# Power of the last group of roots ahead of a rounding, row of the scale from PSUM, late copies of b2 after the early products

## The chip, the cores and the metric

The kernel runs on one core of one Trainium2 chip. The metric is the device time of one execution in microseconds (us). A core has five engines with a queue each: TensorE (PE in the profile, with its weight loads as PEld), VectorE (DVE), ScalarE (ACT), GpSimd (POOL) and SyncE (SP), which here issues DMAs. An engine takes its instructions in order; an instruction that needs the result of another engine waits for a semaphore, and holds up what is queued behind it.

## The reference

```python
xn = _layernorm(x, axis=-1)                                  # x: 8 x 512 x 1024, float32
x = x + attn(xn, w1, w2, b2, sparse_mask) + ffn(xn, weight, bias)

def attn(x, w1, w2, b2, sparse_mask):
    a = jnp.einsum('ds,td->st', w1, w2) * sparse_mask
    y = jnp.einsum('bds,st->bdt', x, a) + b2
    return jax.nn.gelu(y, approximate=False)

def ffn(x, weight, bias):
    w_scale = 448.0 / max(amax(abs(weight)), 1e-12)
    w_q = clip(weight * w_scale, -448, 448).astype(float8_e4m3fn)
    x_scale = 57344.0 / max(amax(abs(x)), 1e-12)
    x_q = clip(x * x_scale, -57344, 57344).astype(float8_e5m2)
    acc = jnp.einsum('bsk,nk->bsn', x_q.astype(float32), w_q.astype(float32))
    return acc * (1.0 / x_scale) * (1.0 / w_scale) + bias
```

The mask is nonzero only near the diagonal (within 70 columns of a block). Both amax values are taken over whole tensors: no row of x can be quantized before the largest normalized value of all 4096 rows is known.

## The kernel before

The 4096 rows are 32 tiles of 128 rows by 1024 columns. Tiles 0 to 15 are "early": they are loaded, normalized in place, transposed (L489), multiplied with the banded, masked attention matrix (L514) and put through gelu (L524) while the statistics and the largest value of all tiles are still being gathered. The last eight early tiles have their transposed copies in one large buffer (`xnt_big`). Tiles 16 to 31 are "late": in the first half they pass only for statistics (L310, or by ScalarE for tiles 16 to 23) and row maxima (L396, `row_max`), and are loaded again after it, normalized into a new tile (L382), transposed, multiplied and put through gelu (L536).

Two scales separate the halves. For each, named "w" and "x", `global_amax` (L706) runs five steps: `amax_rows` on VectorE (L407, one maximum per partition, `x_mine`), a transpose on TensorE into one PSUM row (L412, `pt_x`), `amax_row` on VectorE (L416 finds the largest value, `x_top`; L421 spreads it over a row of 128, `x_row`), a transpose back to 128 partitions on TensorE (L424), and `scale_and_inverse` on VectorE (L428 to L431). x's chain starts once the reciprocal roots of the variances of all groups of tiles are there. The last group, tiles 28 to 31, takes three steps: `variance` on VectorE (L333, `var`), `power` on GpSimd (L337, `r`), and `inverse_root` on VectorE (L343 to L345: `t`, `t`, `rstd`), with `shifts` (L348) behind it; then `late_amax` (L436) scales the row maxima.

The weight is eight chunks of 128 by 1024. Once w's scale is known, ScalarE scales a chunk (L450), VectorE makes a "magic" number for each element (L456, L459), whose addition and subtraction round to three bits, and GpSimd adds and subtracts it, half a chunk at a time (`weight_rounded`: L468 and L469). Chunks 6 and 7 are rounded by VectorE instead (L463, L464).

After both scales are known, VectorE quantizes a transposed tile (L547), TensorE multiplies it with the rounded weight (L554), and VectorE applies scale and bias and adds the rest (L566, L569, L578). 

PSUM holds four tiles of 512 columns for the masked products (`py`), two for the linear part and attention matrix, two for transposes. b2 comes into a `py` tile before the products: by a copy on ScalarE (`preload`, L505) or, for early tiles 11 to 15, by a bias matmul on TensorE (`b2_matmul`, L509). A `py` tile comes free with its gelu. All other tiles of 128 by 1024 come from a pool of 34 slots; an instruction that writes into a slot waits for the last reader of what was there.

The order of the instructions is made by a planner (`Plan`, L116): each step is given an engine, a cost, a rank, the steps that it comes after, and slots that it takes and frees; the planner plays this through in time and emits the steps in the order in which they start. The costs are numbers written by hand, so the plan is not the execution; but each engine's queue has the plan's order.

The lines that the change touches are these, and what they name: `root[TILES - 1]` is the `inverse_root` step of the last group, `products[i]` the last product matmul of early tile i, `rows_op` the step that splits b2 for the bias matmul.

Of the kernel before, what the change touches and what calls it, by code (L numbers as in the profile page):

```python
# [14 lines left out]
ALU = mybir.AluOpType  # L15
AX = mybir.AxisListType

P = 128
# [3 lines left out]
TILES = NT // P  # L22
GROUP = 8
EARLY = 16
# [20 lines left out]
AMAX_EPS = 1e-12  # L45
# [70 lines left out]
class Plan:  # L116
# [8 lines left out]
    def do(self, engine, cost, rank, emit, *args, lag=0.2, after=(), take=(), free=()):  # L125
        after = [op for op in after if op is not None]
        op = Op(engine, cost, rank, lag, after, take, free, emit, args)
        self.ops.append(op)
        return op
# [47 lines left out]
def banded_path(  # L177
# [12 lines left out]
    nc = tc.nc  # L190
# [54 lines left out]
    v = {}  # L245
# [168 lines left out]
    def amax_top(name):  # L414
        v[name, "top"] = top = const.tile([1, 1], F32, name=f"{name}_top")
        nc.vector.tensor_reduce(top, v[name][:1, 0, :], AX.X, ALU.max)  # L416

    def amax_row(name):
        amax_top(name)
        v[name, "row"] = row = const.tile([1, P], F32, tag="amax_row", name=f"{name}_row")  # L420
        nc.vector.tensor_scalar_max(row, v[name, "top"].to_broadcast([1, P]), AMAX_EPS)  # L421

    def amax_back(name):
        nc.tensor.transpose(v[name][:, 1, 0:1], v[name, "row"], ident[:1, :1])  # L424
# [189 lines left out]
    for k in range(4):  # L614
        y = ps_y.tile([P, HALF], F32, tag="y", name=f"py_first_{k}")
# [3 lines left out]
    do = plan.do  # L619
    LOAD, T, V, A, G = "load", "tensor", "vector", "scalar", "gpsimd"  # L620
# [26 lines left out]
    b2_op = do(G, 0.6, 1, load_b2, lag=12.0, after=(attn_ops[0],))  # L647

    attn_mm, attn_ready = [], []
    for sc in range(NC):  # L650
        mm = do(
            T, 3.5, sc * 0.1, attn_matmuls, sc, after=[attn_ops[c] for c in range(sc + 1)],
            take=("f",), free=("slot",),
# [7 lines left out]
    root, shifted = {}, {}  # L661
# [7 lines left out]
    for lo, hi in GROUPS:  # L669
        group = [stat[i] for i in range(lo, hi)]  # L670
        if 0 < lo and hi < TILES:
            op = do(G, 1.7 + 0.16 * (hi - lo), 0, inverse_root_gpsimd, lo, hi, after=group)
        else:
            op = do(V, 0.2, 0, variance, lo, hi, after=group)
            op = do(G, 0.4 + 0.16 * (hi - lo), 0, power, lo, hi, after=(op,))
            op = do(V, 0.6, 0, inverse_root, lo, hi, after=(op,))
        for i in range(lo, hi):
            root[i] = shifted[i] = op
        if lo == 0 or hi == TILES:
            op = do(V, 0.2, 0 if lo == 0 else 99, shifts, lo, hi, after=(op,))  # L680
# [11 lines left out]
    for i in range(EARLY, TILES):  # L692
# [6 lines left out]
        after=[maxima[i] for i in SQUARED] + [root[i] for i in SQUARED],  # L699
# [3 lines left out]
        after=[squared] + [maxima[i] for i in range(TILES)] + [root[i] for i in range(TILES)],  # L703
    )

    def global_amax(name, fp8_max, rank, cols, after, lag=0.1):  # L706
        op = do(V, 0.2, rank, amax_rows, cols, name, after=after, lag=lag)
        op = do(T, 0.4, rank, amax_transpose, name, after=(op,), take=("t",))
        op = do(V, 0.5, rank, amax_row, name, after=(op,))
        op = do(T, 0.3, rank, amax_back, name, after=(op,))  # L710
        return do(V, 0.5, rank, scale_and_inverse, name, fp8_max, after=(op,), free=("t",))
# [6 lines left out]
    rows_op = do(G, 8.6, 2, b2_parts, after=(b2_op, normal[11]))  # L718
    w_known = global_amax("w", E4M3_MAX, 0, w_cols, sums)
    rounded, for_vector = [], []  # L720
    for c in range(NC):
        op = do(A, 1.1, 1, weight_scaled, c, after=(w_known, w_twice[c]))
        op = do(V, 1.4, 1, weight_magic, c, after=(op,), take=("magic",))
        if c in ROUNDED_BY_VECTOR:
            for_vector.append((c, op))
            continue
        op = do(G, 2.55, 1, weight_rounded, c, 0, after=(op, rows_op))
        rounded.append(
            do(G, 2.55, 1, weight_rounded, c, 1, after=(op,), free=("slot", "magic", "twice"), lag=4.0)
        )  # L730
# [7 lines left out]
    products, added = {}, {}  # L738
    evicted = {}
    for i in range(EARLY):  # L740
        in_big = i >= EARLY - NC
        for q in range(2):
            op = do(
                T, 0.52, 10 * i - 11 + q, transposes, i, q,
                after=(settled[i], attn_mm[NC - 1] if in_big else None, evicted.get((i, 0))),
                take=("t",) if in_big or q else ("t", "slot"),
            )
# [10 lines left out]
        op = evicted[i, 1]  # L758
        ends = []
        for piece in band_pieces():  # L760
            op = do(
                T, 0.4, 10 * i, product_matmul, i, *piece, lag=0.1 if not piece[-1] else 0.2,
                after=(op, evicted[i, 0], attn_ready[piece[0]], pre[piece[1]]),
            )
# [4 lines left out]
        op = do(LOAD, 2.5, 200 + 10 * i, lambda: None, lag=0.0, after=(*ends, late))  # L769
# [11 lines left out]
    normal_late, evicted_late, pre_late, added_late = {}, {}, {}, {}  # L781
    last_piece = {}
    for n, j in enumerate(range(EARLY, TILES)):
        s = step[n]
        fetched[j] = do(
            LOAD, 1.4, 195 + 10 * n, load_x, j, lag=2.0, take=("slot", "late"), after=(maxima[j],)
        )
        xn = do(A, 1.2, 100 + s, normalize_late, j, after=(fetched[j], shifted[j], known if n > 1 else root[TILES - 1]), take=("slot",))
        if n == 0:
            for q in range(2):  # L790
                op = do(
                    T, 0.52, 900 + q, transposes, j, q, after=(xn, evicted_late.get((j, 0))),
                    take=("t",) if q else ("t", "slot"), free=("slot",) if q else (),
                )
                evicted_late[j, q] = do(A, 0.55, 50, evict_transposed, j, q, after=(op,), free=("t",))
        normal_late[j] = xn
        for h in range(2):
            pre_late[j, h] = do(A, 0.55, 60 + s, preload, j, h, after=(b2_op,), take=("y",))
    linear = None
    for s, k in enumerate(steps):  # L800
        rank = 1000 + 10 * s
        j = EARLY + k if k < EARLY else None
        if j is not None:
            quantized[k] = do(
                V, 1.3, 100 + s, quantize, k, after=(x_known, products[k], evicted[k, 1]),
                take=("quant",), free=("slot",) if k < EARLY - NC else (),
# [4 lines left out]
        op = linear  # L811
        sums_k = []
        for kind, args in interleaved(j is not None, nxt is not None):
            if kind == "product":
                h = args[1]
                op = do(
                    T, 0.33, rank, product_matmul, j, *args, lag=0.0,
                    after=(op, evicted_late[j, 0], evicted_late[j, 1], pre_late[j, h]),
                )
                if args[-1]:  # L820
                    last_piece[j, h] = op
            elif kind == "transpose":
                c, = args
                q, first, last = c // (NC // 2), c % (NC // 2) == 0, c % (NC // 2) == NC // 2 - 1
                op = do(
                    T, 0.13, rank, transpose_one, nxt, c, lag=0.0, after=(op, normal_late[nxt]),
                    take=(("t", "slot") if c == 0 else ("t",)) if first else (),
                    free=("slot",) if c == NC - 1 else (),
                )
# [4 lines left out]
            else:  # L834
                h, c = args
                op = do(
                    T, 0.215, rank, linear_matmul, k, h, c, lag=0.0,
                    after=(op, quantized[k], *(rounded if s == 0 else ())),
                    take=("f",) if c == 0 else (), free=("quant",) if (h, c) == (1, NC - 1) else (),
                )  # L840
# [3 lines left out]
        if j is not None:  # L844
            for h in range(2):
                g = do(
                    A, 0.55, 20 + s, gelu_late, j, h, after=(last_piece[j, h],),
                    take=() if h else ("slot",), free=("y",),
# [6 lines left out]
                take=("quant",), free=("slot",),  # L855
            )
        totals = []
        for h in range(2):
            ready = added_late[k, h] if k >= EARLY else added[k]
            if s == TILES - 1:  # L860
                op = do(G, 1.27, 20 + s, add_bias, k, h, after=(ready, bias_op))
                op = do(V, 0.8, 10 + s, total_at_once, k, h, after=(op, sums_k[h], known), free=("f",))
# [11 lines left out]
    for sc in range(NC):  # L874
        m = do(
            LOAD, 1.4, 300 + sc, load_mask, sc, lag=2.0, take=("slot", "stream"),
            after=(known, stored[2 * sc + 3]),
# [4 lines left out]
    op = do(V, 0.2, 300, amax_rows, out_cols, "o", after=checks)  # L882
    op = do(T, 0.3, 5000, amax_transpose, "o", after=(op,), take=("t",))
# [248 lines left out]
def layernorm_masked_product_fp8_linear(tc, x, w1, w2t, b2, mask, wt, bias, out):  # L1132
    nc = tc.nc
    with tc.tile_pool(name="flag", bufs=1) as pool:
        flag = pool.tile([1, 1], I32, name="flag")
        banded_path(tc, x, w1, w2t, b2, mask, wt, bias, out, flag)
        general = nc.values_load(
            flag,
            min_val=0,
            max_val=1,  # L1140
            skip_runtime_bounds_check_because="a comparison gives 0 or 1",
        )
    with tc.If(general != 0):
        general_path(tc, x, w1, w2t, b2, mask, wt, bias, out)
# [35 lines left out]
```

## Time and profile before

| | us |
|---|---|
| median of 3 runs | 320.34 |
| the runs | 320.34, 320.46, 318.3 |
| the profiled execution | 318.67 |
| its span in the profile | 316.9 |
| TensorE busy | 291.6 |
| VectorE busy | 231.7 |
| ScalarE busy | 158.2 |
| GpSimd busy | 134.4 |

The profile is of one execution. A busy share is an average over stages: about 50 us of loading with the attention matrix and the first tiles, then until about 122 us the rest of the early tiles beside statistics, maxima and the weight's rounding, then the linear part of all tiles and the products of the late ones. In lines of the timelines the columns are start and length in us, engine, line of the kernel, operation, what is written and read with its shape, and the count; brackets give the engine's idle time just before, and what is taken to have ended it. In lines of waits: who waited for whom, the total, the number of times, and the longest. Matmuls are pipelined, so a matmul's own length overlaps the next one's; in the chain of waits each has only the time until the next one starts.

How the 40 slices of the span look (busy tenths of each engine):

```profile
PE   2779889998999979999999999999999999999992
DVE  3489698999999969646577677767767755766581
```

### The profile page before, as it was taken

Reading aid. Unit: us, or ns where it says so; the run is one execution under the profiler, and the core shown is the slowest. Engines: PE = TensorE matmul, PEld = TensorE weight load, DVE = VectorE, ACT = ScalarE, POOL = GpSimd, SP = SyncE. Lnnn points to the kernel's source line nnn. Section 1 sums busy time; section 2 is a strip of 40 time slices with the busy share of each in tenths; the row PEclk is TensorE's granted clock in tenths of the full one; section 3 lists DMA queues with packets and bytes.
Section 4 is the critical chain, followed back from the end, with each engine's and each line's share of the span. In section 5 each row is a group of like instructions: output and inputs, shape, how many; then the busy total and the mean of one; then the engine's idle time right before and its main releaser. Section 6 shows DMA issues by size and latency. Waiting matters only on the chain.

```text
span 316.9 us, 4342 instructions
## 1 busy us (share of the span) xinstructions
PE 291.6 (92%) x1555; PEld 217.9 (69%) x1555; DVE 231.7 (73%) x342; ACT 158.2 (50%) x255; POOL 134.4 (42%) x165
## 2 busy tenths in 40 slices
PE   2779889998999979999999999999999999999992
PEld 0757668896998867876676676676667667667650
DVE  3489698999999969646577677767767755766581
ACT  1368369584999973744344334523524443452110
POOL 3151708988488789666202311311330231131160
PEclk9999999999999998999999999999999999999999
DMA  7999999999535746999999986653153322221313
GB/s 248 407 383 378 391 392 390 395 420 418 222 110 221 238 161 112 208 209 271 296 283 299 379 334 223 243 186 147 66 199 133 115 109 114 103 96 66 134 67 141
DMA packets 28365, 73.74 MB, mean 233 GB/s; under 512 B 3376, under 2 KB 11568, under 8 KB 28336
## 3 DMA queue, kind: packets, MB, share of 16 engines
q1 hardware_dynamic: 20992, 47.17, 40.2%
q0 software_dynamic: 2592, 9.44, 14.7%
q10 hardware_dynamic: 4752, 16.78, 13.1%
q8 instruction: 14, 0.23, 0.3%
q14 instruction: 15, 0.12, 0.1%
HBM read 56.60 MB, written 16.78 MB: 232 GB/s over the span
## 4 chain that ended last, share of the span: by engine, by line
PE 61%; DVE 19%; DMA 10%; SPq 5%; POOL 1%; issue 1%; ACT 0%; DVEq 0%
PE pf L554 35%; PE py L514 21%; DMA w<-in_w_dram 8%; DVE row_amax L396 6%; PE pt L489 5%; SPq L259 4%; DVE st L310 4%; DVE magic L456 2%; DVE w_cols L444 2%; DMA x<-in_x_dram 2%; DVE magic L459 2%; SPq L250 1%; PE pa L293 1%; DVE mean_var L311 1%; DVE xnt_big L501 1%
## 5 line engine op out<-in xcount | busy, mean ns | idle before, releaser
L554 PE MATMUL pf<-wq,xqts 128*128 128x512 bf16 x512 | 149.5, 379 | 0.0
L514 PE MATMUL py<-attn,xnt 128*128 128x268 f32 (+2 forms) x480 | 117.3, 340 | 1.6 <-ACT py L505 0.9
L514 PEld LDWEIGHTS py<-attn,xnt 128*128 128x128 f32 x480 | 86.7, 190 | 24.1 <-ACT py L505 1.1
L539 POOL TENSOR_TENSOR x<-x,gelu 128x512 f32<-128x512 f32 x32 | 40.6, 1270 | 126.2 <-ACT gelu L536 124.7
L566 DVE SCALAR_TENSOR_TENSOR pf<-pf,descale,bias_bc 128x512 f32<-128x512 f32 x62 | 46.9, 756 | 54.2 <-PE pf L554 54.2
L554 PEld LDWEIGHTS <-xqts 128*128 128x128 fp8e5 x512 | 50.6, 101 | 23.6 <-issue 0.2
L536 ACT ACTIVATE gelu<-py 128x512 f32<-128x512 f32 x32 | 19.1, 597 | 76.5 <-PE py L514 73.1
L569 DVE TENSOR_TENSOR x<-pf,x 128x512 f32<-128x512 f32 x62 | 42.9, 692 | 4.4 <-DVE pf L566 0.5
L396 DVE TENSOR_REDUCE row_amax<-x 128x1 f32<-128x1024 f32 x32 | 37.6, 1201 | 4.5 <-POOL x L391 4.1
L293 PE MATMUL pa<-w_sb,w 128*128 128x268 f32 (+1 forms) x128 | 31.3, 402 | 9.5 <-DMA w_sb<-in_w2t_dram 9.5
L310 DVE BATCH_NORM_STATS2 st<-x 128x6 f32<-128x512 f32 x48 | 30.3, 673 | 8.2 <-DMA x<-in_x_dram 8.2
L293 PEld LDWEIGHTS pa<-w_sb,w 128*128 128x128 f32 x128 | 25.5, 207 | 14.8 <-issue 11.3
L498 ACT COPY xnt<-pt 128x512 f32<-128x512 f32 x48 | 27.2, 581 | 16.1 <-PE pt L489 16.1
L514 PE MATMUL py<-attn,xnt_big 128*128 128x198 f32 (+2 forms) x160 | 34.7, 353 | 0.0
L489 PE MATMUL pt<-ident,xn 128*128 128x128 f32 x128 | 33.9, 273 | 0.0
L505 ACT COPY py<-b_bc 128x512 f32<-128x512 f32 x54 | 31.9, 600 | 1.0
L514 PEld LDWEIGHTS py<-attn,xnt_big 128*128 128x128 f32 x160 | 27.5, 196 | 3.4 <-issue 0.8
L489 PEld LDWEIGHTS pt<-ident,xn 128*128 128x128 f32 x128 | 18.0, 141 | 13.9
L382 ACT ACTIVATE xn<-x,shift,rstd 128x1024 f32<-128x1024 f32 x16 | 19.9, 1241 | 11.1 <-DVE x L569 9.1
L524 ACT ACTIVATE x<-py 128x512 f32<-128x512 f32 x32 | 18.5, 600 | 11.2 <-PE py L514 11.1
L547 DVE TENSOR_SCALAR xqts<-xnt,x_scale 128x1024 fp8e5<-128x1024 f32 x24 | 21.2, 888 | 0.0
L489 PE MATMUL pt<-ident,x 128*128 128x128 f32 x128 | 18.8, 274 | 1.9 <-ACT xnt L498 0.9
(100 smaller groups left out, 236.2 us busy)
## 6 DMA issues: line engine op xcount, KB each, us to landing
x<-in_x_dram SPq DMA_DIRECT2D x48, 512.0 KB, 7.6
out_dram<-x ACTq DMA_DIRECT2D x31, 512.0 KB, 2.8
w<-in_wt_dram SPq DMA_DIRECT2D x16, 512.0 KB, 8.5
x<-in_x_dram POOLq DMA_DIRECT2D x16, 512.0 KB, 18.5
w<-in_w_dram SPq DMA_DIRECT2D x8, 512.0 KB, 9.0
mask<-in_mask_dram SPq DMA_DIRECT2D x8, 512.0 KB, 7.9
w_sb<-in_w2t_dram SPq DMA_DIRECT2D x6, 512.0 KB, 10.7
attn<-in_mask_dram SPq DMA_DIRECT2D x6, 134.0 KB, 9.2
```

The costliest lines, as they stand in the source:

```text
L293: nc.tensor.matmul(pt[:, : hi - lo], w1_sb[:, c, :], w2_sb[:, c, lo:hi], start=(c == 0), stop=(c == NC - 1),)
L310: nc.vector.bn_stats(st[:, h, :], xs[i][:, half(h)])
L396: nc.vector.tensor_reduce(row_amax[:, i : i + 1], xs[i], AX.X, ALU.max, apply_absolute_value=True)
L489: nc.tensor.transpose(pts[i, q][:, j, :], xn[:, c * P : (c + 1) * P], ident)
L498: nc.scalar.copy(xnts[i][:, q * (NC // 2) : (q + 1) * (NC // 2), :], pts.pop((i, q)))
L505: nc.scalar.copy(pys[i, h], b2_bc[:, half(h)])
L514: nc.tensor.matmul(pys[i, h][:, lo - h * HALF : hi - h * HALF], xnts[i][:, sc, :], attn[:, sc, lo - band(sc)[0] : hi - band(sc)[0]], start ...
L539: nc.gpsimd.tensor_add(xs[i][:, half(h)], xs[i][:, half(h)], gelus[i][:, half(h)])
L547: nc.vector.tensor_scalar(v["quant"][:, xqts[i]], xnts.pop(i), v["x"][0], E5M2_MAX, ALU.mult, ALU.min, saturate=False)
L554: nc.tensor.matmul(v["pf", i, h], v["quant"][:, xqts[i], c, :], wq[:, c, half(h)], start=(c == 0), stop=(c == NC - 1),)
L566: nc.vector.scalar_tensor_tensor(pf, pf, v["descale"], v["bias"][:, half(h)], ALU.mult, ALU.add)
L569: nc.vector.tensor_add(res[:, half(h)], pf, res[:, half(h)])
```

## The change

Three edits. In `amax_row`, the row is no longer the one value `top`, read 128 times, but the maximum of the PSUM row, `top` and the small constant: since `top` is the largest of that row, the row comes out the same. The input tensor is now in PSUM, and `top` is a scalar operand. `amax_row` serves both scales.

In the plan, the first half of chunk 4's rounding on GpSimd also comes after the last group's `inverse_root`. And the copies of b2 for late tiles come after the last product matmul of early tile 14 (`EARLY - 2`), where before they only came after the load of b2 and a free `py` tile.

```diff
@@ amax_row
         amax_top(name)
         v[name, "row"] = row = const.tile([1, P], F32, tag="amax_row", name=f"{name}_row")
-        nc.vector.tensor_scalar_max(row, v[name, "top"].to_broadcast([1, P]), AMAX_EPS)
+
+        nc.vector.tensor_scalar(row, v[name][:1, 0, :], v[name, "top"], AMAX_EPS, ALU.max, ALU.max)
@@ the plan: rounding of the weight, c is the chunk
-        op = do(G, 2.55, 1, weight_rounded, c, 0, after=(op, rows_op))
+        op = do(G, 2.55, 1, weight_rounded, c, 0, after=(op, rows_op, root[TILES - 1] if c == 4 else None))
@@ the plan: copies of b2 for late tile j
-            pre_late[j, h] = do(A, 0.55, 60 + s, preload, j, h, after=(b2_op,), take=("y",))
+            pre_late[j, h] = do(A, 0.55, 60 + s, preload, j, h, after=(b2_op, products[EARLY - 2]), take=("y",))
```

The number of instructions stays the same on each engine. As the planner plays the new conditions through, the queues differ from before in the stretch around x's scale. GpSimd: `power` stands ahead of the first half of chunk 4's rounding, not behind it. VectorE: `t`, `t`, `rstd` and `shift` stand ahead of the last row maximum (tile 31), not behind it, and the magic of chunk 6 stands behind x's scale, not ahead of `x_top`. ScalarE: tile 16's first copy of b2 moves from ahead of chunk 7's scaling to behind the first gelu of tile 15; normalizing tile 19 moves ahead of the last gelu of tile 14. TensorE: the transpose of `x_mine` comes one pair of matmuls earlier in the order, the one back three pairs earlier, and the eight transposes of tile 16 come behind the last early product.

## The prediction

> **What bounds the kernel now.** I read the chain that ended last first, then TensorE's waits, then the stretch around the largest wait.
>
> ```profile
> span 316.9 us, 4342 instructions
> PE 61%; DVE 19%; DMA 10%; SPq 5%; POOL 1%; issue 1%; ACT 0%; DVEq 0%
> PE pa L293 <- DMA w_sb<-in_w2t_dram: 9.5, 4, 6.3
> PE pt_x L412 <- DVE x_mine L407: 2.2, 1, 2.2
> PE pt_w L412 <- DVE w_mine L407: 0.7, 1, 0.7
> PE pt_x L424 <- DVE x_row L421: 0.6, 1, 0.6
> PE pt_w L424 <- DVE w_row L421: 0.6, 1, 0.6
> ```
>
> Loading ends the waits up to some 52 us; then the chain lies on VectorE until 122 us, and from there it is TensorE without a gap to 310.8. So what comes before 122 us counts by how far it moves TensorE's restart, and a step saved beside the dense matmuls later counts nothing. The four waits above that belong to the two scales (x and w) are all that TensorE still loses to them. The timelines of VectorE and GpSimd say why:
>
> ```profile
> 77.13 0.84 DVE L421 TENSOR_SCALAR w_row<-w_top 1x128 f32<-1x128 f32 x1
> 110.17 1.16 POOL L468 TENSOR_TENSOR w<-w,magic 128x512 f32<-128x512 f32 x1 [1.18 <-DVE var L333]
> 111.40 1.16 POOL L469 TENSOR_TENSOR wq<-w,magic 128x512 bf16<-128x512 f32 x1
> 112.52 1.04 POOL L337 TENSOR_TENSOR r<-var,neg_half 128x4 f32<-128x4 f32 x1
> 113.60 1.12 DVE L343 TENSOR_TENSOR t<-r 128x4 f32<-128x4 f32 x1 [2.40 <-POOL r L337]
> 114.77 1.16 POOL L469 TENSOR_TENSOR wq<-w,magic 128x512 bf16<-128x512 f32 x1
> 114.95 1.01 DVE L345 SCALAR_TENSOR_TENSOR rstd<-t,r 128x4 f32<-128x4 f32 x1
> 115.88 0.68 DVE L456 TENSOR_SCALAR magic<-w 128x1024 int16<-128x1024 int16 x1
> 117.24 1.62 DVE L456 TENSOR_SCALAR magic<-w 128x1024 int16<-128x1024 int16 x1
> 120.38 1.64 DVE L421 TENSOR_SCALAR x_row<-x_top 1x128 f32<-1x128 f32 x1
> ```
>
> Tiny VectorE steps (0.16 us when alone, L344) last over 1 us when they start beside a GpSimd add, and end with that add: t until 114.7, rstd until 115.96. L456 needs 0.64 to 0.69 alone and up to 1.62 beside an add. And x's row waits in VectorE's queue behind a whole magic step (117.24 to 120.15). The windows add the clock:
>
> ```profile
> 114.19:117.60 3.41, 1.17 (x10) 1.01 (x9) 3.31 (x9) 3.05 (x4) 2.12 (x3) 1.00 0.09 36
> 117.60:121.02 3.42, 3.42 (x10) 2.41 (x10) 3.35 (x4) 0.20 (x1) 3.34 (x4) 0.50 0.00 0
> ```
>
> (length; busy PE, PEld, DVE, ACT, POOL with counts; clock; DMA.) After a 2.25 us wait TensorE runs 3.41 us at half clock, which costs half of it, 1.7 us.
>
> **Row of w from PSUM.** The step lasted 0.84, as GpSimd's normalize (76.69 to 77.9) held it; alone it would be about 0.16 to 0.27 (L344; L416, which reads that PSUM row in 0.27 while GpSimd works). No row shows this form reading PSUM. Bounds: 0.16, and 0.84 if it is held as before; I take 0.25, near L416, as both read the same 128 numbers: 0.6 saved. TensorE's 0.58 wait for it goes, and VectorE is full from here to 110 us (9.8 to 9.9 of every 10 us), with GpSimd's adds started by its magic steps, so both move up together. I pass on all 0.6 to x_mine; the low bound is 0, if GpSimd's adds take it back. **−0.6.**
>
> The Trainium skill, "VectorE: DVE Perf Modes", section "Why PSUM operands drop a tier", says that an operand in PSUM rules out the mode that uses both SBUF read ports; by it both rows would be free of GpSimd, as I take them, and no run here shows it yet.
>
> **Power ahead of the rounding.** In the changed queue r follows var (ready 110.07) instead of two adds: it ends near 111.2, not 113.56, and the two adds of chunk 4's first half move behind it. But the changed VectorE queue then has t, t, rstd, shift, row_amax, magic of chunk 5 (L456, L459), then the amax. t and rstd again meet the two adds and end with them, near 112.4 and 113.6, 2.35 us earlier. shift (0.16) is moved in here from a free place and row_amax (1.13 a step), which before filled the wait for r, now follows: they end between 114.95 and 116.0. The second half's adds run 113.6 to 116.0, so L456 is held to 116.0 and ends about where it did (116.56). The 2.35 us are lost again in front of it. Bounds: −0.4, if L456 slips between the two adds near 114.8, and +0.2. Row_amax ends just behind that gap, so I take **0.**
>
> **Row of x, and the magic behind it.** Chunk 6's magic (2.9 us as it ran) now stands behind x's scale. x_mine reaches TensorE at the same place (117.47 less what is saved above); the transpose takes 0.28, x_top 0.27, the row 0.25: ready near 118.4. TensorE has, between the transposes, one pair of 70 columns, one 128x512 bias matmul and one pair of 198 (0.17, 0.21, 0.34 in the chain): doubled by the half clock 1.45 us, so it arrives near 119.0 and waits for nothing: 0.64 saved, in a stretch at full clock. The pair of 70 columns ran before the wait and now runs after it: 0.17 back. If the row were held as before, it would end with the adds near 120, and TensorE would wait 1.0. So −0.64 to +0.5; I take **−0.47.** The magic of chunk 6, descale, first quantize and L463/L464 end by 125.4 to 126.2 (before: 126.2), chunk 7 by 131.4; the linear matmul that reads chunk 7 comes past 133, so that cover holds.
>
> **Late copies.** Tile 16's first copy (112.93, 0.59) goes from idle ScalarE time to the end of the early tiles, where four 0.6 us copies now share ScalarE with the last gelus. The product matmuls get the fourth PSUM buffer; but TensorE shows no wait for one from 122 to 131 us, so this gains nothing. The planner also puts tile 16's eight transposes behind the last early product instead of among them, with the eviction (L498) behind the last gelu. From the end of that product: gelu starts 0.25 later (as 122.55 to 122.86 shows), L498 0.48 behind it, lasting 0.58: 1.3; TensorE fills 0.88 with transposes and 0.22 with the first linear matmul. It waits 0.28, where it waited for nothing. Bounds 0 and 0.6. The three later copies end by 2.8 us, the first reader of tile 16's second half comes at 4.3. No DMA is added; one accumulating load changes places with one add. **+0.28.**
>
> Sum: −0.6 + 0 − 0.47 + 0.28 = −0.8. The profiled execution took 318.67 (span 316.9 and 1.77 around it): 317.9. That execution is 1.7 under the median of the runs, 320.34; the runs and it (318.3, 318.67, 320.34, 320.46) mean 319.44, so I expect 318.6 in the middle of such a spread.
>
> **Rivals.**
> - *The clock stays up.* If the long wait falls across two of the clock's windows, or shrinks (L456 slipping in), the half-clock stretch is not entered: 1.7 more, −2.5, 316.9. For: the window before the drop held 1.17 us of work, and cut elsewhere none would. Against: the wait itself is not shortened in my sum (2.25 + 0.17). Chance 0.2. The Trainium skill, "TensorE: Matmul & The Clock Gate", Part 1, lets the clock fall after a whole idle window of about 3.4 us, free-running against the kernel. By the first half the 2.25 us wait would not have halved it at all; the trace disagrees. The second half makes it luck, execution by execution.
> - *PSUM frees nothing.* Both rows stay held: no 0.6, and at x 1.0 of wait for 0.64: +0.36 + 0.17 + 0.28 = +0.8, about 320.2. For: no such row in the trace. Against: L416 and L566 (746 to 759 ns in all 62, GpSimd busy or not) read PSUM undisturbed. Chance 0.12.
> - *Slower: ScalarE held behind VectorE.* normalize of tile 19 (1.24 us) now stands ahead of the last three gelus, and its slot comes free with L464 of chunk 6; before it stood behind the eviction. It must start by about 127.0 for the last gelu to be on time, with L464 expected at 125.7. If quantize, L463 and L464 are each held by a GpSimd op (0.8 + 1.16 + 1.16 = 3.1), all behind it, TensorE's late products too, loses 1.8: −0.8 + 1.8 = +1.0, 320.4. It decides once L464 ends past 128. Against: GpSimd's adds are over at 123.1, and its DMA issues behind them left L463 at 1.21. Chance 0.08.
>
> **Numbers.** My case has 0.6: 318.6, by itself 317.4 to 319.9. The range takes in the clock rival and the two above: 316.6 to 320.6. A difference under 1% (317.1 to 323.5 around the median) can't be told from no change. Faster by more needs the clock rival or the low end of the spread: 0.22. Slower by more has only a much longer hold of ScalarE: 0.05. Within: 0.73.
>
> **What would show it.** Right: w's and x's rows at 0.15 to 0.3; TensorE's waits for the rows gone; r ending near 111 with L456 of chunk 5 still held to 116 and the x_mine wait above 2 us; a new wait under 0.6 on the eviction of tile 16. Wrong: x_mine's wait well under 2 us or no half-clock window (then the power step, or luck, gave more), rows still near 1 us, or a wait of ScalarE on L464 in front of the last gelus.

## The result, and the profile after

| | before | after |
|---|---|---|
| median of 22 runs each | 319.99 | 317.73 |
| lowest and highest | 318.28, 321.17 | 316.87, 319.18 |
| the profiled execution | 318.67 | 317.78 |
| its span | 316.9 | 316.0 |

The ratio is 0.9949, with a 95% interval of 0.9933 to 0.9965: half a per cent faster (the two medians by themselves stand at 0.9929). The two profiled executions are 0.9 us apart, the medians 2.26. That the medians differ by more than the profiles is part of the result, and the second profile of the kernel before, further down, shows where such a difference can lie.

In the changed kernel lines from 421 on are one higher. TensorE's waits for the scales, and the engines' shares of the chain that ended last (line, releaser; total, times, longest):

```profile
PE 61%; DVE 16%; DMA 10%; SPq 5%; ACT 2%; issue 2%; POOL 2%; POOLq 0%; DVEq 0%; ACTq 0%
```

```profile
PE pt_x L412 <- DVE x_mine L407: 2.3, 1, 2.3
PE pt_w L412 <- DVE w_mine L407: 0.7, 1, 0.7
PEld py L515 <- ACT xnt L499: 0.5, 1, 0.5
```

Both waits for a row are gone, the wait for `x_mine` is as long as before, and a short one for the eviction of tile 16 has come (0.5 is the weight load's; TensorE itself lost 0.23 there, below). VectorE's timeline of the same execution:

```profile
76.98 0.34 DVE L422 TENSOR_SCALAR w_row<-pt_w,w_top 1x128 f32<-1x128 f32 x1
110.59 1.12 DVE L343 TENSOR_TENSOR t<-r 128x4 f32<-128x4 f32 x1 [1.15 <-POOL r L337]
111.95 1.01 DVE L345 SCALAR_TENSOR_TENSOR rstd<-t,r 128x4 f32<-128x4 f32 x1
112.99 1.08 DVE L348 SCALAR_TENSOR_TENSOR shift<-mean_var,rstd 128x4 f32<-128x4 f32 x1
114.00 1.21 DVE L396 TENSOR_REDUCE row_amax<-x 128x1 f32<-128x1024 f32 x1
115.12 0.71 DVE L457 TENSOR_SCALAR magic<-w 128x1024 int16<-128x1024 int16 x1
116.41 0.19 DVE L407 TENSOR_REDUCE x_mine<-row_amax 128x1 f32<-128x32 f32 x1
117.37 0.34 DVE L422 TENSOR_SCALAR x_row<-pt_x,x_top 1x128 f32<-1x128 f32 x1
```

Both rows take 0.34. In the kernel before, the last step of this chain and the first late product of TensorE were here:

```profile
117.14 0.19 DVE L407 TENSOR_REDUCE x_mine<-row_amax 128x1 f32<-128x32 f32 x1
131.03 0.57 PE L514 MATMUL py<-attn,xnt 128*128 128x198 f32 x2
```

`t` starts 3 us earlier than before (110.59 for 113.60), but `x_mine` only 0.73 earlier (116.41 for 117.14): `t`, `rstd` and `shift` last 1 us each, and the row maximum now stands behind them. The windows around the wait (length; busy PE, PEld, DVE, ACT, POOL with counts; clock; DMA) and GpSimd's timeline:

```profile
114.14:117.55 3.41, 1.09 (x8) 0.69 (x6) 2.85 (x7) 1.18 (x3) 2.27 (x2) 1.00 0.00 0
117.55:120.97 3.42, 3.42 (x10) 2.48 (x9) 2.96 (x6) 1.40 (x2) 3.26 (x5) 0.50 0.33 24
```

```profile
109.52 1.04 POOL L337 TENSOR_TENSOR r<-var,neg_half 128x4 f32<-128x4 f32 x1 [1.17 <-DVE var L333]
110.55 1.15 POOL L469 TENSOR_TENSOR w<-w,magic 128x512 f32<-128x512 f32 x1
111.77 1.16 POOL L470 TENSOR_TENSOR wq<-w,magic 128x512 bf16<-128x512 f32 x1
112.90 1.15 POOL L469 TENSOR_TENSOR w<-w,magic 128x512 f32<-128x512 f32 x1
```

`t`, `rstd` and `shift` end with the first three adds (111.70, 112.93, 114.05). The half-clock stretch is there with the same length. Last, the end of the early tiles on ScalarE and TensorE:

```profile
124.88 2.36 ACT L382 ACTIVATE xn<-x,shift,rstd 128x1024 f32<-128x1024 f32 x2
129.31 0.58 ACT L499 COPY xnt<-pt 128x512 f32<-128x512 f32 x1
129.49 0.38 PE L555 MATMUL pf<-wq,xqts 128*128 128x512 bf16 x1
129.94 0.60 PE L515 MATMUL py<-attn,xnt 128*128 128x198 f32 x2
```

The first late product (129.94; 131.03 before) starts 0.23 behind the end of the matmul in front of it (0.22 after 129.49, by the next issue in the dense stretch). The last step of VectorE starts at 309.78, before at 310.84. So a measure for all that follows: **from the first late product to that last step all kernels with the queues' order of before or of the change take 179.7 to 179.9 us.** What an edit does lies in two steps ahead of it: from w's transposition (L412, `pt_w`) to x's (`pt_x`), and from x's to the first late product.

| profile of | w's to x's transposition | x's to the first late product | last step | clock after the x_mine wait |
|---|---|---|---|---|
| before | 41.53 | 13.56 | 310.84 | half, 117.6 to 121.0 |
| before, second profile | 41.53 | 15.24 | 311.91 | full; half after x's row |
| after | 40.97 | 13.19 | 309.78 | half |
| row only | 41.05 | 12.87 | 309.75 | half |
| row of w only | 41.06 | 13.57 | 310.38 | half |
| row of x only | 41.53 | 12.27 | 310.03 | full |
| row and copies | 41.05 | 13.08 | 309.69 | full |
| copies only | 41.62 | 15.99 | 313.56 | half, two stretches |
| change + filling | 40.90 | 12.38 | 309.17 | full |
| change + tile 19 | 40.96 | 12.93 | 309.70 | half |
| change + both | 40.89 | 11.44 | 308.04 | full |
| row + both | 40.95 | 12.36 | 309.57 | full |

Each entry is a difference of two starts in the trace. w's transposition itself begins between 75.33 and 76.44: the loading varies by 1.1 us from execution to execution, which is why the last step alone is a worse measure than the two steps.

### The profile page after: what moved, and what is told of

Its sections match the earlier page's. It is cut to its first block, busy times and chain, and to the rows that moved or that the text cites. A ratio compares the mean times of both kernels' runs of the same rounds, so it can differ in the third digit from the quotient of the medians.

```text
span 316.0 us, 4344 instructions
## 1 busy us (share of the span) xinstructions
PE 291.8 (92%) x1555; PEld 217.9 (69%) x1555; DVE 231.7 (73%) x342; ACT 158.7 (50%) x255; POOL 134.2 (42%) x165
## 4 chain that ended last, share of the span: by engine, by line
PE 61%; DVE 16%; DMA 10%; SPq 5%; ACT 2%; issue 2%; POOL 2%; POOLq 0%; DVEq 0%; ACTq 0%
PE pf L555 35%; PE py L515 21%; DMA w<-in_w_dram 8%; DVE row_amax L396 5%; PE pt L490 4%; SPq L259 4%; DVE st L310 3%; DVE w_cols L445 2%; DMA x<-in_x_dram 2%; SPq L250 1%; DVE magic L457 1%; PE pa L293 1%; DVE magic L460 1%; ACT xn L382 1%; POOL w L469 1%
```

## The experiments

Times are medians over five rounds, with the ratio to the kernel before run in the same set on the same chip; the median of before moved from 319.0 to 320.2 between sets. Small differences between ratios of different sets are therefore to be read with care, and the steps of the table stand beside them.

**The row alone** (the first edit of the change, the others undone).

> Only the row from PSUM, all queues in the order of before. Theory (the row gives both gains): w's row 0.84 to 0.34, all of VectorE up to x_mine 0.5 to 0.6 earlier; x's row still starts behind chunk 6's magic, near 119.5, but lasts 0.34 instead of 1.64, so TensorE no longer waits 0.64 for it: -1.1 to -1.2 us in all, as much as the whole change in the profile (-1.06). Rival (x's gain comes from the magic that the power step moved out of the way): the wait of 0.64 stays, -0.5 us.

Measured: 317.57, ratio 0.9947 [0.9926, 0.9969], the same as the whole change. The queues are those of before, so x's row stands behind chunk 6's magic, and it still takes 0.34:

```profile
116.84 1.62 DVE L456 TENSOR_SCALAR magic<-w 128x1024 int16<-128x1024 int16 x1
118.49 1.26 DVE L459 TENSOR_SCALAR magic<-magic 128x1024 bf16<-128x1024 bf16 x1
119.98 0.34 DVE L421 TENSOR_SCALAR x_row<-pt_x,x_top 1x128 f32<-1x128 f32 x1
```

L459, whose input and output are both in SBUF, is held to 1.26 beside GpSimd's adds (0.43 alone); the row that reads PSUM, next to it, is not.

**The late copies alone** (the third edit).

> Only the late copies of b2 behind the last product of tile 14. Theory: nothing gained, as TensorE waits for no py tile between 122 and 131 us; a wait of 0.2 to 0.3 us for the eviction of tile 16: 0 to +0.3 us. Rival (the fourth py tile sets the early products free): -0.3 to -0.6 us, with less waiting of TensorE before 131 us.

Measured: 320.15, ratio 1.0024 [1.0, 1.0048]: alone the edit gains nothing. In the profiled execution, which was the slowest of the twelve (321.54), TensorE waits 1.4 us for x's row, and the half clock lasts two stretches (118.9 to 125.7); 0.65 us go to the eviction of tile 16, more than the 0.2 to 0.3 expected.

**The power alone** (the second edit).

> Only the power step ahead of the rounding. The planner now also emits tile 16's and 17's copies of b2 and tile 16's evictions ahead of the gelus of tiles 14 and 15, and so the products of tiles 14 and 15 among the linear part. Theory: r ends 2.3 us earlier, x_mine does not (held in front of chunk 5's magic), x's row held or not as GpSimd stands; 0 to -0.6 us if the early products fit in later without a gap, up to +1 us where they make TensorE wait. Rival (power is what the change lives on): x_mine's step 1 us or more earlier, -1 us or more.

Measured: 321.38, ratio 1.0077 [1.0057, 1.0097], slower. TensorE's waits:

```profile
PE pt_x L412 <- DVE x_mine L407: 2.3, 1, 2.3
PE pf L554 <- DVE wq L464: 1.5, 1, 1.5
PE pt L489 <- ACT xn L382: 0.7, 1, 0.7
PE py L509 <- ACT x L524: 0.7, 1, 0.7
```

The wait for `x_mine` is not shorter, and w's transposition lies 41.53 ahead of x's, as before. The three waits below it are new; they end between 121 and 131 us. The last step of VectorE starts at 313.22, 2.4 later than before. With this one condition the planner emits tile 16's and 17's copies of b2 and tile 16's evictions ahead of the gelus of tiles 14 and 15 on ScalarE, and spreads the products of those tiles into the linear part. The instructions are the same; the order of two other engines is worse.

**The change without the late copies** (row and power).

> The whole change without the late copies. Theory (the third edit's work is to keep the planner from emitting tile 16's and 17's copies ahead of the early products of tiles 14 and 15, which the power step brought on): the power step alone was at 1.0077; with the row 0.5 us less (w's; at x there was no wait left to save): ratio 1.005 to 1.007, slower than before. Rival (the third edit is idle, the row decides): ratio 0.995 as the whole change.

Measured: 321.47, ratio 1.0079 [1.005, 1.0109]. w's row brings `x_mine` forward here too (40.96), but two of the three new waits are there, 0.7 us each, the half clock lasts two stretches (117.5 to 124.3), and the last step starts at 313.05. What the row gains is gone with the order that the power edit makes; with the late copies added it is the whole change, 0.9949. So the third edit is worth 1.2% (by the medians) to 1.3% (by the ratios) here, by undoing that order; by itself it costs 0.2%, which is hardly clear of noise.

**The change without the power** (row and copies).

> The whole change without the power step: r and chunk 6's magic stay where they were before. Theory (the power step brought nothing of its own): x_mine's step where the row alone has it, x's row ready near 120.4 as there, when TensorE just arrives; the wait for tile 16's eviction 0.2 to 0.6 us; as fast as the whole change within 0.3 us (ratio to before 0.994 to 0.996). Rival (power's 2.3 us, or the magic moved behind x's scale, is worth something): 0.5 us or more slower than the whole change (ratio 0.9965 or more).

Measured: 318.36, ratio 0.9967 [0.994, 0.9994], between the row alone and no change. The ratio itself is on the rival's side, and the interval holds both, so by the times it stays open whether the power step brings something of its own. In the profiled execution the clock stays at 1.00, and still the first late product comes 13.08 us after x's transposition, as in the executions at half clock: TensorE waits 1.0 us for x's row (behind chunk 6's magic) and 0.65 for tile 16's eviction.

**The row for w only, and for x only.**

```diff
+if name == "w":      # the other experiment: "x"
+    nc.vector.tensor_scalar(row, v[name][:1, 0, :], v[name, "top"], AMAX_EPS, ALU.max, ALU.max)
+else:
     nc.vector.tensor_scalar_max(row, v[name, "top"].to_broadcast([1, P]), AMAX_EPS)
```

> The row from PSUM for w alone, x's row as before, all queues as before. Theory: the 0.5 to 0.6 us that w's row gives up reach x_mine undiminished, and the wait for x's row (0.64) stays: -0.5 us, ratio 0.998. Rival (GpSimd's adds take the 0.5 us back, and x's row is the whole gain): ratio 1.000.

> The row reads PSUM for x only; w's row is spread from the SBUF scalar as before, all queues as before. Theory A (each row carries its own part): w's row stays at 0.84 us with a wait of TensorE of about 0.6, x's row falls from 1.64 to 0.34, and only the second part of the gain is there: 0.6 us of some 1.1, ratio about 0.998. Theory B (the row of x carries nearly all, and what comes earlier at w is lost again before x's scale): ratio 0.995, the same as with both rows. The row of w alone gave 1.0005 [0.9975, 1.0035], which leans to B but holds both.

Measured: w only 319.77, ratio 1.0005 [0.9975, 1.0035]; x only 317.84, ratio 0.9942 [0.9918, 0.9965]. By the times x's row carries all of it. The profiles say what each does: with w's row alone the way to x's transposition is 0.47 shorter and what follows is unchanged (13.57); with x's row alone it is the other way round (41.53 and 12.27). 0.47 us is 0.15%, which the interval of the first ratio holds. x's row is worth more than the 0.64 us that TensorE waited for it in the first profile, and that profile could not show why. The single times point the same way: with w's row only the twelve runs still fall apart, five up to 318.44 and seven from 319.6, while with x's row only eleven of twelve are at 318.41 or below.

**The kernel before, profiled once more.** Its 22 runs beside the changed kernel fall in two heaps, 10 from 318.28 to 318.59 and 12 from 319.96 to 321.17; the profile that the prediction had (318.67) is of the lower one. In the other sets a few runs of it lie in between (319.02, 319.33, 319.74 among them).

> The kernel before itself, once more, to have a second profile of it: its times fall in two heaps, near 318.5 and near 320.3, and the profile at hand is of the lower one. If the profiled execution falls in the upper heap, the step from x_mine to the first late product shows where the 1.8 us lie: theory A, a second half-clock stretch of 3.4 us (1.7 us) at the wait for x's row; theory B, a longer loading, with everything behind it shifted and that step still at 13.6. If it falls in the lower heap the origin stays open.

Measured: one round, in which the kernel stood at 1.0008 [0.9976, 1.0041] to itself, although the medians of its 8 and 9 runs were 320.17 and 318.97. The profiled execution took 320.12, of the upper heap. TensorE's waits, its matmul behind x's row, and windows of the length of a half-clock stretch:

```profile
PE pt_x L424 <- DVE x_row L421: 2.3, 1, 2.3
PE pt_x L412 <- DVE x_mine L407: 2.2, 1, 2.2
```

```profile
119.77 1.63 DVE L421 TENSOR_SCALAR x_row<-x_top 1x128 f32<-1x128 f32 x1
```

```profile
121.46 0.22 PE L424 MATMUL pt_x<-ident,x_row 1*128 1x1 f32 x1 [2.32 <-DVE x_row L421]
```

```profile
115.56:118.97 3.41, 2.11 (x11) 1.64 (x11) 3.34 (x7) 1.38 (x2) 2.35 (x2) 1.00 0.00 0
118.97:122.38 3.41, 1.09 (x7) 0.86 (x6) 2.96 (x7) 0.13 (x1) 3.33 (x4) 0.98 0.37 55
122.38:125.79 3.41, 3.41 (x12) 2.79 (x11) 3.38 (x5) 1.59 (x2) 3.41 (x7) 0.52 1.01 171
```

Neither of the two theories written down is right. There is one half-clock stretch, as in the lower heap, but at another place. The `x_mine` wait is as long (2.23) and the clock does not fall behind it. TensorE, at full clock, is through its few matmuls sooner and then waits 2.32 us, not 0.64, for the row that is held; and this second wait halves the clock. The difference of the waits, 2.32 − 0.64 = 1.68, is the difference of the two profiles from x's transposition to the first late product (15.24 − 13.56 = 1.68). So x's row from PSUM gains little where the clock has already fallen, and more where it has not: there TensorE waits 1.03 instead of 2.32, and no stretch at half clock follows, as in the profile with x's row only, where the step is 12.27. This is one profile of each heap; that all the runs of the upper heap are of this kind is not shown.

```profile
121.25 0.22 PE L427 MATMUL pt_x<-ident,x_row 1*128 1x1 f32 x1 [1.03 <-DVE x_row L422]
```

**Filling the x_mine wait.** Nine matmuls on a tile of zeros are put ahead of x's transposition into the PSUM tile that this then overwrites; everything else is the changed kernel.

```diff
+for k in range(9 if name == "x" else 0):
+    nc.tensor.matmul(pt, zeros[:, :P], zeros, start=True, stop=True)
```

> The whole change, and nine 128x512 matmuls of zeros into the same PSUM tile ahead of the transpose of x_mine (9 x 0.215 = 1.9 of the 2.3 us that TensorE waits there). Theory (the half-clock stretch costs 1.7 us and comes from this wait): the clock stays at 1.00 until the last matmul, -1.4 to -1.7 us against the whole change, so -2.3 to -3.3 us against before. Rival (the stretch follows something else, or zeros do not count as work): the window at 0.50 stays, 0 to +0.2 us against the whole change.

Measured: 317.09, ratio 0.995 [0.9926, 0.9973]; by the ratio no faster than the change (0.9949), and short of the 2.3 to 3.3 us expected. Two of the seven runs are at 318.25 and 318.27; neither was profiled. In the profiled execution the clock stays at 1.00 up to the last product. The filling in TensorE's timeline:

```profile
114.53 2.10 PE L413 MATMUL pt_x<-zeros 128*128 128x512 bf16 x8
```

One profile does not show that the filling did it, since with x's row only, and with row and copies, the clock stays up without filling. The traces together do. In each of the fourteen profiles (those of the table, power alone, row and power) the places at which the clock changes lie a whole number of steps of 3.413 us apart (before: 117.60 and 315.57 are 58 steps apart). So every trace can be cut into windows at these steps, from the first full clock, at 12 to 17 us, to the last change. The clock fell behind all 23 windows in which TensorE was busy for 1.37 us or less, and behind none of the 1194 at full clock in which it was busy for 1.59 or more. The windows that hold the wait for `x_mine`:

| profile of | window from | TensorE busy in it, of 3.41 | clock behind it |
|---|---|---|---|
| before | 114.19 | 1.17 | half |
| before, second profile | 112.01 and 115.43 | 2.61 and 1.98 | full |
| row of x only | 113.77 and 117.18 | 1.94 and 2.28 | full |
| row and copies | 112.73 and 116.15 | 1.79 and 2.28 | full |
| after | 114.16 | 1.10 | half |
| change + filling | 114.16 | 3.05 | full |

In the last two rows the windows lie at the same place, and only the filling differs: the half-clock stretch does come from the wait, where one window holds nearly all of it. But of its 1.7 us only 0.81 arrive (12.38 for 13.19). TensorE then waits for ScalarE (lines two higher than before):

```profile
125.58 1.24 ACT L382 ACTIVATE xn<-x,shift,rstd 128x1024 f32<-128x1024 f32 x1 [0.23 <-DVE wq L466]
```

```profile
129.32 0.60 PE L516 MATMUL py<-attn,xnt 128*128 128x198 f32 x2 [0.79 <-ACT xnt L500]
```

Normalizing tile 19 stands ahead of three gelus, and its slot comes free with chunk 6's last rounding step: the mechanism of the prediction's slower rival.

**Tile 19 later, alone and with the filling.** ScalarE normalizes tile 19 behind the last early product.

```diff
-after=(fetched[j], shifted[j], known if n > 1 else root[TILES - 1])
+after=(fetched[j], shifted[j], products[EARLY - 1] if n == 3 else None, known if n > 1 else root[TILES - 1])
```

> The whole change, and the normalizing of tile 19 on ScalarE planned after the last early product, without the filling matmuls. The half-clock stretch behind the wait for x_mine stays. If the clock and ScalarE are two limits of nearly the same height, taking away ScalarE's alone gives only the 0.23 us that TensorE lost in front of tile 16's first product: ratio 0.994 to 0.995, about the whole change. If ScalarE alone were the limit: ratio near 0.991, as with the filling added.

> The whole change with nine matmuls of zeros ahead of x_mine's transpose, and the normalize of tile 19 planned behind the last early product. With the filling alone the clock stayed at 1.00, but TensorE then waited 0.8 us for tile 16's eviction, behind tile 19's normalize, which waited for chunk 6's rounding. Theory: that wait goes, 0.6 to 0.8 us less than with the filling alone: 316.3 to 316.5, ratio 0.990 to 0.993. Rival (VectorE's rounding of chunks 6 and 7 holds TensorE next): 0 to 0.2 us less, ratio 0.995, with a wait on L464 or on a quantize.

Measured: alone 317.59, ratio 0.9915 [0.9886, 0.9944]; with the filling 316.1, ratio 0.9906 [0.9871, 0.9941]. The ratio of the first is lower than expected, but its median is only 0.14 under that of the changed kernel, measured in another set, and its profile 0.26 (12.93 for 13.19, the 0.23 in front of tile 16's product among it): most of that ratio is a high median of before in that set (320.2). Its nine runs are two heaps as well: two at 316.05 and 316.24 with a mean clock of 0.995 and 0.998, seven from 317.35 up at 0.993 or less. With the filling all six runs are from 315.51 to 316.93. So the clock and ScalarE were two limits of nearly the same height: one taken away gives 0.81 or 0.26 us in the profile, both give 1.75. This version, the change with both additions, is the fastest here: all but one of its runs (316.93) are below the lowest of the changed kernel (316.87).

**The row with both additions, in the order of before** (no power edit, no late copies).

> Only the row from PSUM (power and late copies as before the change), with the nine filling matmuls and with tile 19 behind the last early product: no half-clock stretch and ScalarE free, but x's row stands in VectorE's queue behind chunk 6's magic. If the change's other two edits are worth nothing even when these two limits are gone: ratio 0.9906, as the whole change with the same two additions. If the magic's place costs what TensorE then waits for x's row (1.0 us in the run without the power edit where the clock stayed up): ratio about 0.993 to 0.994.

Measured: 317.07, ratio 0.9907 [0.9874, 0.994]. By the ratio the two other edits would be worth nothing; the profile has the wait that the second theory expected,

```profile
PE pt_x L426 <- DVE x_row L423: 1.1, 1, 1.1
```

and 12.36 us where the whole change with the same additions has 11.44 (the profiled execution was the slowest of six, 317.6). The medians, 317.07 and 316.1, differ in the same way but are from different sets. I take the magic's place behind x's scale to be worth some 0.9 us once nothing else is late; the times alone do not prove it.

## Why the prediction was right, and where it was not

The forecast of 318.6 is 0.9 above the median, inside its range, and the sum for the profiled execution (−0.8, 317.9) is 0.12 off the one measured (317.78). That it is so close is in part luck. The step up to x's transposition lost 0.56 (forecast −0.6 for w's row, 0 for the power) and the step behind it 0.37 (forecast −0.47 + 0.28 = −0.19); loading was 0.16 shorter in this execution (75.78 for 75.94), and what lies behind the last step of VectorE about as much longer.

**Row of w: right, a little too large.** The row took 0.34, not 0.25, so it saved 0.5. That nearly all of it reaches `x_mine` is shown: the step from w's to x's transposition is 0.47 to 0.64 shorter in every profile of the table with w's row from PSUM, and as before without it. The Trainium skill, "VectorE: DVE Perf Modes", section "Why PSUM operands drop a tier", lets an operand in PSUM rule out the mode with both SBUF read ports; the trace agrees, with both rows at 0.34 while GpSimd works (normalizing beside w's, adding beside x's) against 0.84 and 1.64 from SBUF. So the rival that PSUM frees nothing has fallen.

**Power: right in its own place, wrong as an edit.** r ended at 110.56 and `x_mine` came no earlier for it: 41.53 with the power alone, as before, and 40.97 with the whole change against 41.05 with the row alone. The 0 was right, but the time was lost in another place than forecast. `t` and `rstd` were held, as I had them; `shift`, which I had at 0.16, lasted 1.08 beside the third add, and the row maximum came behind it. L456 of chunk 5, which I had held to the end of the adds, was hardly held (0.71). What failed is the step that treated the three edits as terms to be added. The edit alone makes the kernel 0.8% slower, through the order that the planner then gives ScalarE and TensorE, and no row of the profile of before could have shown it; playing the plan with each edit alone would have.

**Row of x: right mechanism, mis-sized.** "Waits for nothing" is what the profile after shows, but by a hair: the row ends at 117.71, TensorE's transposition back starts at 117.76. The forecast had 0.6 to spare (118.4 and 119.0), since it let all matmuls in between run at half clock; the half clock began only at 117.58. In the profile with row and power, 0.19 of wait is left there. The step that failed is "0.64 saved": it carried TensorE's wait from one execution to all of them, and 0.64 is its length only after the clock has fallen. Where it had not, in the second profile of before, the same held row cost 2.32. With the rows alone, at half clock, the step from x's transposition on is 0.69 shorter than before (12.87 for 13.56), where the term had −0.47.

**The spread.** "I expect 318.6 in the middle of such a spread" took the scatter of the four times for noise that the changed kernel would have too. Its upper values are the upper heap of the kernel before, in whose one profile the held row makes the difference, and that heap is all but gone: with the rows alone all 8 runs are within 316.95 to 317.93, and 18 of the 22 of the changed kernel are at 318.45 or below. The middle of the spread stood 0.77 above the profiled execution (319.44 for 318.67); this is most of the 0.9 us by which the forecast is high.

**Late copies: right by size in the profile, wrong in worth.** The prediction had 0.28 (its terms as written, with 0.25 up to the gelu, give 0.21; between 122.55 and 122.86 lie 0.31, which gives 0.27); TensorE lost 0.23 in front of tile 16's first product, and the whole change is 0.32 behind the row alone in that step (13.19 for 12.87). "This gains nothing" holds for the edit by itself (1.0024), but not beside the power edit, whose order it repairs.

**The clock rival.** It put the price of the half-clock stretch at 1.7 us, −2.5 in all. Filling the wait shows the price that counts: 0.81, since ScalarE is next. In the kernel before a clock that stays up at `x_mine` even led to the longer time. The condition of the rival was right: where the wait falls across two windows, each keeps 1.79 us of work or more, and the clock stays up; this was so in three of the eleven profiles without filling. The Trainium skill, "TensorE: Matmul & The Clock Gate", Part 1, has the window free-running, so that where a wait falls differs from run to run; the two profiles of one kernel agree: the same 2.2 us wait left the clock at 0.50 in one and at 1.00 in the other.

**ScalarE behind VectorE.** In the changed kernel tile 19's normalize started without a wait, so the rival did not decide; but it stood ready, and is the first thing in the way once the clock is repaired.

**What stays open.** Four of the 22 runs of the changed kernel are at 318.96 to 319.18 with a mean clock of 0.983 to 0.985, which is room for a second half-clock stretch; none of them was profiled, so where it lies is not shown. In the profiles of the copies alone and of row and power the half clock lasted two windows instead of one, although TensorE was busy for 2.04 and 3.10 us of the first; with the power alone 2.73 were enough to end it. What ends a half-clock stretch is not shown by these runs. Nor do the times settle what the power edit is worth beside the other two.

## What to carry to other kernels

When the times of the kernel before fall in two heaps, find out which heap the profile is from, or take a second profile, before a wait is priced: the same wait can be 0.64 in one execution and 2.32 in the next. Where a planner makes the order, an edit's worth is not a term of its own; compare the queues of each edit alone and together. And a small VectorE step on the path that may read its operand from PSUM is, as here, no longer held by GpSimd, which needs no reordering at all. Before a wait is blamed for a slow clock or filled, cut the trace into the clock's windows and count the busy time in each.

## What the runs showed of the hardware that had not been expected

A window need not be idle for the clock to fall. In the fourteen profiles windows of 3.41 us with 1.08 to 1.37 us of TensorE's work were followed by clock 0.50, and none with 1.59 or more was. So a wait of 2.2 us halves the clock or not, by where it falls: in the first profile of before one window held it and kept 1.17 us of work, in the second it was cut in two and the window with the larger part kept 1.98. The 128x512 matmuls on zeros (nine in the kernel, eight in the trace, 2.1 us) in front of the transposition brought the window from 1.10 to 3.05, and the clock stayed at 1.00: work on zeros counts as work.

The two rows of 1x128, with the tensor in PSUM and a pointer scalar, took 337 to 340 ns in every profile that has them, each time with GpSimd at work beside them. The same step read from SBUF took 827 to 892 ns for w's row, beside GpSimd's normalizing, and 1633 to 1639 for x's beside an add. With the power edit alone x's row took 293 ns from SBUF, from 117.52 on, as one add ended (117.74) and before the next began (117.81): the form in SBUF is not slow, it is exposed.
